# Token mixer of a Macaron block: its front in two strands, gate and convolutions as strands, PSUM banks from one pool, keys in quarters

## Chip, core and metric

The kernel runs on one core of a Trainium2 chip. The metric is the device time of one execution in microseconds (us). PE is the TensorE matmul engine (PEld its weight loads), DVE VectorE, ACT ScalarE, POOL GpSimd, SP the SyncE queue that issues most transfers. Each engine works through its own instructions in order; semaphores make it wait for the others.

## What is computed

A Macaron block on x of 16 x 256 tokens of 128 numbers: half a mixture-of-experts layer, a token mixer, half a mixture-of-experts layer, each on a layer norm and added to x. All in float32.

```python
x = x + 0.5 * ffn(layernorm(x))
x = x + attn(layernorm(x))
x = x + 0.5 * ffn(layernorm(x))
```

The mixer `attn`, cut to what matters (4 heads of 32, chunks of 32 tokens):

```python
q, k, v = (silu(causal_conv4(h @ W)) for W in (Wq, Wk, Wv))
beta = sigmoid(h @ Wb)
q, k = l2norm(q), l2norm(k)
attn = -(k * beta) @ k.T * strict_lower          # per chunk, 32 x 32
for i in range(1, 32):
    attn[i, :i] += attn[i, :] @ attn[:, :i]      # inverse of a triangular system
attn = attn + eye(32)
u, w = attn @ (v * beta), attn @ (k * beta)
for each chunk:                                  # scan over 8 chunks
    a_loc = q @ k.T * incl_lower
    u = u - w @ S
    delta = q @ S + a_loc @ u
    S = S + k.T @ u
ms = mix(conv3(v), conv15(v), conv31(v)) @ channel_mixer_w
features = concat(h, mean|ms|, mean|delta|, mean|v|)
wts = softmax(gelu(features @ W1 + b1) @ W2 + b2)
o = wts[0] * ms + wts[1] * delta + wts[2] * v
return rmsnorm(o) @ Wo
```

## The kernel before

The program has three stages. The first routes all tokens, scatters them by expert through DRAM and runs 2 x 8 expert passes (L456 to L533). The second is the token mixer (L670 to L1178). The third repeats the expert passes for the second half layer, whose routing has been done inside the mixer.

The mixer treats the tokens in four groups (g = 0 to 3) of 4 sequences x 256 tokens. For each group there are five Python generators, called strands:

- `front` (L724): adds the last expert output to x (load y from `back`, L731), layer norm, transposes into hT, projections pj for keys and queries (L719, four taps each, two halves), beta, the norms pn of k and q from squares sq. Then, in the same strand, the keys are spread by heads into `kh` by small copies on SP (L801, two halves of four copies), the products pa (L813) are masked into acomp and alc, acomp is transposed to sys, `inv` is set to the identity on POOL (L839) and the 32 x 32 systems are inverted on DVE, column after column (L846, L851, 31 steps of two instructions). Last, tcomp goes to the zero-padded tz on ACT (L872), and pw and pu (L881) give wT and uT.
- `values` (L890): projection of v, 16 copies that lay v out with lags in `vlag` (L909), transposition to vtok.
- `scan` (L918): 8 chunks, each pc, ui, pS, S, po, with DVE between the matmuls.
- `mixing` (L990): the lagged convolutions as 26 rounds of four 32-column matmuls (pms, L1010), channel mixing pk, then the gate: features, hidden layer ph, logits plg, softmax, the weighted sum o, norm, oT, output matmul pyo added to x.
- `routing` (L1168): routing of the group for the second expert stage, and 16 indirect stores by POOL (`dispatch`, L435).

What sets the order: a planner, `Weave.run` (L92), takes the steps of all strands, with an estimated length per step from `pe`, `dve`, `act` and `dma` (L62 to L75), and issues at each turn the step that could start first; the compiler's scheduler takes the resulting program as its order of preference. `("wait", key)` holds a strand until another has called `weave.mark(key)`; `("hold", "R")` takes the one bank R. In `front`, the wait for `("front", g - 1)` at L727 stands ahead of everything, and that mark is set at L888, after pw and pu of the group before. The products pa wait for the scan of the group before (L794).

[...]In the mixer F has two (front and values), V two (mixing), and C, O (scan outputs), S (scan state) and R (routing and logits) one each (L670). In SBUF, the ring f4 (two buffers, front) holds y, xn, sq, acomp, kb and vb, the ring b4 (three) the tiles of mixing; kq has two buffers, alc, sys, inv, wT, uT and ktok one.

Of the kernel before, what the change touches and what calls it, by code (L numbers as in the profile page):

```python
# [26 lines left out]
VPAD = 28  # L27
# [34 lines left out]
def pe(cols, *after):  # L62
    return PE, max(0.06, 0.0014 * cols), after


def dve(n, *after):
    return DVE, 0.15 + 0.00104 * n, after


def act(n, *after):  # L70
    return ACT, max(0.45, 0.12 + 0.00091 * n), after
# [6 lines left out]
class Weave:  # L78
# [4 lines left out]
    def __init__(self):  # L83
        self.done, self.held = {}, set()
# [4 lines left out]
    def let_go(self, key):  # L89
        self.held.discard(key)  # L90

    def run(self, strands):  # L92


        free, now = {}, [[s, next(s)] for s in strands]

        def start(step):
            if step[0] == "wait":
                return 0.0 if step[1] in self.done else None
            if step[0] == "hold":  # L100
                return 0.0 if step[1] not in self.held else None
            engine, _, after = step

            return max(
                [free.get(engine, 0.0)]
                + [t + (0.0 if e == engine else 0.2) for e, t in filter(None, after)]
            )

        while now:
            at, i = min((t, i) for i, (_, step) in enumerate(now) if (t := start(step)) is not None)  # L110
            strand, step = now[i]
            if step[0] == "wait":
                answer = self.done[step[1]]
            elif step[0] == "hold":
                self.held.add(step[1])
                answer = None
            else:
                engine, length, _ = step

                free[engine] = at + (0.1 if engine == SP else length)  # L120
# [8 lines left out]
def macaron_kernel(ctx: ExitStack, tc: tile.TileContext, x_in, consts, wts, w1b, wexp, out):  # L129
# [7 lines left out]
    banks = {}  # L137

    def psum_for(phase, **tags):
# [4 lines left out]
        for tag, n in tags.items():  # L144
            banks[tag] = (p, n)

    def bank(tag, name):
        p, n = banks[tag]
        return p.tile([P, 512], F32, tag=tag, bufs=n, name=name)

# [6 lines left out]
    psum_for("1", A=4, B=2, R=1)  # L157
# [23 lines left out]
    weave = Weave()  # L181
# [72 lines left out]
    def transposed(dst, src, tag, name, t=None, by_batch=False):  # L254


        for half in range(2):
            pt = bank(tag, f"pt_{name}_{half}")
            for q in range(4):
                t1 = yield pe(128, t)  # L260
# [7 lines left out]
            else:  # L268
                nc.scalar.copy(dst[:, half * 512 : (half + 1) * 512], pt)
        return t2  # L270

    def by_token(dst, mov, w32, p, at0, n, t=None):

        for b in range(4):
            t1 = yield pe(n / 4, t)
# [10 lines left out]
    class Routing:  # L286


        def __init__(self, layer, pool, bufs):
# [7 lines left out]
            self.last = None  # L297
# [5 lines left out]
        def route(self, g, tag, t=None):  # L303
# [10 lines left out]
            yield "hold", "R"  # L314
            pr = bank("R", f"pr_{nm}")
            t = yield from by_token(
                lgt.rearrange("p n r -> p (n r)"), lambda b: xnT[:, b, :],
                gate32.rearrange("p i e -> p (i e)"), pr, 0, L, t,
            )
            weave.let_go("R")  # L320
# [51 lines left out]
            yield "hold", "R"  # L372
            pp = bank("R", f"pp_{nm}")
# [46 lines left out]
            weave.let_go("R")  # L420

        def in_order(self, sent):

            sent = sent.ins if hasattr(sent, "ins") else sent
# [112 lines left out]
    for g in range(NG):  # L537
        weave.run([r1.route(g, "A")])
# [131 lines left out]
    psum_for("2", F=2, V=2, C=1, O=1, S=1, R=1)  # L670
# [7 lines left out]
    vlag = ap_.tile([P, 4, 4, VPAD + L], F32, name="vlag")  # L678
    nc.gpsimd.memset(vlag[:, :, :, : VPAD + 3], 0.0)
    kh = ap_.tile([P, H, 4 * P], F32, name="kh")  # L680
# [9 lines left out]
    def fring(name):  # L690
        return big("f4", name, 2)

    def bring(name):
        return big("b4", name, 3)
# [16 lines left out]

    def projection(g, w, half, t):

        pj = bank("F", f"pj{w}_{g}_{half}")
        hT = held[g]["hT"]
        for i in range(KQ):
            t1 = yield pe(512, t)
# [6 lines left out]
    def front(g):  # L724
# [4 lines left out]
        t = yield dma(3.0)  # L729
# [6 lines left out]
        t = yield from layernorm(xn, g, f"a{g}", t)  # L736
        hT = f["hT"] = hTs[g % 2]
        t = yield from transposed(hT[:, :, KQ - 1 :], xn, "F", f"a{g}", t, by_batch=True)
        weave.mark(("hT", g), t)

        kq = f["kq"] = ap_.tile([P, 2, NC * P], F32, tag="kq", bufs=2, name=f"kq_{g}")
        tk = {}
        for i in range(2):
            for half in range(2):
                pj, t1 = yield from projection(g, i, half, t)
                tk[i, half] = yield act(512, t1)
                nc.scalar.activation(
                    by_chunk(kq[:, i, half * 512 : (half + 1) * 512]), pj, AF.Silu
                )

        pb = bank("F", f"pb_{g}")
# [3 lines left out]
            wb32.rearrange("p i h -> p (i h)"), pb, 0, L, t,  # L755
        )
        beta = small("beta", [NC, H], f"beta_{g}", 1)
# [5 lines left out]
        pn = bank("F", f"pn_{g}")  # L763
        r32 = small("r32", [2, NC, 32], f"r32_{g}", 1)
        for i in range(2):
            sq = fring(f"sq{i}_{g}").rearrange("p (b l) -> p b l", b=4)
            t1 = yield act(1024, tk[i, 1])
            nc.scalar.activation(
                sq.rearrange("p b (n c) -> p b n c", c=CH), by_chunk(kq[:, i, :]), AF.Square
            )  # L770
            t1 = yield from by_token(
                r32[:, i].rearrange("p n r -> p (n r)"), lambda b: sq[:, b, :],
                blk32.rearrange("p i h -> p (i h)"), pn, i * L, L, t1,
            )
        r2 = small("r2", [2, NC, H], f"r2_{g}", 1)
# [15 lines left out]
        weave.mark(("bv", g), t2)  # L791


        yield "wait", ("scan", g - 1)  # L794
        acomp = fring(f"acomp_{g}")
        alc = f["alc"] = ap_.tile([P, NC, H, CH], F32, tag="alc", name=f"alc_{g}")
        for half in range(2):
            for h in range(H):
                rows = slice(h * DH, (h + 1) * DH)
                t1 = yield dma(2.5, tk[0, half])  # L800
                nc.sync.dma_start(  # L801
                    out=kh[rows, h, :], in_=kq[rows, 0, half * 512 : (half + 1) * 512]
                )
            for q in range(2):
                n0 = 4 * half + 2 * q
                pa = bank("F", f"pa_{g}_{n0}")
                for n in (n0, n0 + 1):
                    for h in range(H):
                        t2 = yield pe(64, t1)
                        c0 = ((n - n0) * H + h) * 2 * CH  # L810
                        for b in range(4):
                            at0 = (n % 4) * P + b * CH
                            nc.tensor.matmul(  # L813
                                pa[b * CH : (b + 1) * CH, c0 : c0 + 2 * CH],
                                lhsT=kh[:, h, at0 : at0 + CH],
                                rhs=kq[:, :, n * P + b * CH : n * P + (b + 1) * CH],
                                start=True, stop=True,
                            )
                pv = pa.rearrange("p (m i e) -> p m i e", i=2, e=CH)
                ta = yield dve(256, t2, tb)  # L820
                nc.vector.tensor_tensor(
                    m32(acomp)[:, n0 * H : (n0 + 2) * H, :], pv[:, :, 0, :],
                    nbk[:, n0 : n0 + 2, :].rearrange("p n h -> p (n h)").unsqueeze(2).to_broadcast(
                        [P, 2 * H, CH]
                    ),
                    ALU.mult,
                )
                yield dve(256)
                nc.vector.tensor_tensor(
                    alc[:, n0 : n0 + 2].rearrange("p n h c -> p (n h) c"), pv[:, :, 1, :],  # L830
                    incl32.unsqueeze(1).to_broadcast([P, 2 * H, CH]), ALU.mult,
                )

        sys_ = big("sys", f"sys_{g}").rearrange("p (e c) -> p e c", e=CH)
        yield dve(1024)
# [442 lines left out]
```

## Time and profile before

Three executions took 1179.99, 1186.2 and 1199.26 us; the median is 1186.2 us.

| | |
|---|---|
| profiled execution | 1185.7 us, its span 1183.7 us, mean TensorE clock 0.891 |
| busy over the span | PE 918.1 us (78%), DVE 494.8 (42%), ACT 353.8 (30%), POOL 296.3 (25%) |
| routing and expert stage 1 | 0 to 346 us |
| token mixer | 346 to 931 us: first group to 444, then some 133 us for each further one, last scan ends at 864 |
| expert stage 2 | 931 to 1184 us |
| costliest mixer groups | pms L1010 112.3 us, pj L719 94.9 us (PE), inverse L846 and L851 42.3 and 42.4 us (DVE) |

In windows of the trace, each row gives for a stretch the busy time of each engine with its instructions, the granted TensorE clock (1.00 is full speed) and the share of time in which the transfer engines were busy. The chain of waits follows the end of the program back from each instruction to what released it. "issue" is time in which an engine waited for nothing that the profile shows.

### The profile page before, as it was taken

The page shows a single profiled execution, that of the slowest core. Times are in us where ns is not written, and L with a number is a line of the kernel's source. Part 1 is how long each engine was busy: PE and PEld are TensorE (multiplying, and loading weights), DVE is VectorE, ACT ScalarE, POOL GpSimd, SP SyncE. Part 2 cuts the span into 40 slices and gives each one's busy share as a digit, 9 for nine tenths or more (in the row PEclk, how much of TensorE's full clock was granted, in tenths as well). Part 3 has the DMA queues.
Part 4 walks back from the last instruction along what each step waited for, and adds up shares of the span by engine and source line. Part 5 has one row for each costly group of instructions (what it writes and reads, how often), then busy time and mean ns, then how long its engine had stood idle before and what let it go on. Part 6 is the DMA issues. An engine that isn't in the chain of part 4 may idle for free.

```text
span 1183.7 us, 19481 instructions
## 1 busy us (share of the span) xinstructions
PE 918.1 (78%) x7721; PEld 613.5 (52%) x7721; DVE 494.8 (42%) x1346; ACT 353.8 (30%) x694; POOL 296.3 (25%) x312
## 2 busy tenths in 40 slices
PE   4348888999949858977597958977644699989992
PEld 2236666777733434443454435443432477767772
DVE  7422323443330563359325644359243133343332
ACT  6213212222214133622345223622232122222220
POOL 2623555333340000002300050002201433323331
PEclk9668999999988987989698978989675799999997
DMA  9451643533110301030103011030002233342314
GB/s 331 170 214 61 190 164 125 201 110 94 57 36 9 82 1 28 9 73 17 40 10 81 2 37 28 13 69 18 22 1 86 69 108 101 100 161 90 102 32 153
DMA packets 40491, 97.43 MB, mean 82 GB/s; under 512 B 8560, under 2 KB 17239, under 8 KB 40400
## 3 DMA queue, kind: packets, MB, share of 16 engines
q1 hardware_dynamic: 29888, 76.78, 21.1%
q0 software_dynamic: 9216, 16.87, 4.3%
q10 hardware_dynamic: 1296, 2.54, 0.6%
q8 instruction: 61, 1.00, 0.3%
q14 instruction: 30, 0.25, 0.1%
HBM read 47.65 MB, written 40.29 MB: 74 GB/s over the span
## 4 chain that ended last, share of the span: by engine, by line
PE 56%; DVE 20%; issue 12%; DMA 5%; ACT 2%; POOL 2%; another core or an unknown queue 1%; SPq 0%; POOLq 0%; DVEq 0%; ACTq 0%
PE pg L494 11%; PE py L511 11%; PE pu L499 11%; PE pj L719 8%; DVE inv L851 3%; DVE add L846 3%; PE pms L1010 3%; DMA y<-back 3%; PE ptx L483 1%; POOL disp L439 1%; ACT tz L872 1%; DVE ye L515 1%; PE pw L881 1%; PE pu L881 1%
## 5 line engine op out<-in xcount | busy, mean ns | idle before, releaser
L439 POOL DMA_INDIRECT disp<-row,send x128 | 128.4, 1003 | 474.5 <-DVE inv L851 337.6
L523 POOL DMA_INDIRECT back<-ye,xd x160 | 156.3, 977 | 312.6 <-DVE ye L515 259.6
L505 DVE TENSOR_TENSOR hT<-pu,sg 128x320 f32<-128x320 f32 x256 | 125.5, 491 | 181.5 <-PE pu L499 117.0
L494 PE MATMUL pg<-xdT,we 128*128 128x320 f32 x512 | 185.3, 444 | 1.2 <-issue 1.1
L499 PE MATMUL pu<-xdT,we 128*128 128x320 f32 x512 | 181.9, 437 | 4.3 <-issue 3.6
L504 ACT ACTIVATE sg<-pg 128x320 f32<-128x320 f32 x256 | 111.8, 437 | 197.8 <-PE pg L494 133.6
L511 PE MATMUL py<-we,hT 128*128 128x128 f32 x1280 | 151.1, 276 | 8.9 <-DVE hT L505 8.4
L511 PEld LDWEIGHTS py<-we,hT 128*128 128x128 f32 x1280 | 149.0, 192 | 16.0 <-DVE hT L505 9.9
L499 PEld LDWEIGHTS pu<-xdT,we 128*128 128x128 f32 x512 | 97.7, 192 | 48.0 <-issue 8.0
L494 PEld LDWEIGHTS pg<-xdT,we 128*128 128x128 f32 x512 | 95.8, 193 | 43.7 <-ACT xdT L486 5.2
L1010 PE MATMUL pms<-vlag,lagw 128*32 128x512 f32 x832 | 112.3, 594 | 3.8 <-DMA vlag<-vbl 3.2
L719 PE MATMUL pj<-hT,wc 128*128 128x512 f32 x192 | 94.9, 624 | 1.2 <-ACT hT L264 0.9
L486 ACT COPY xdT<-ptx 128x384 f32<-128x384 f32 x32 | 15.3, 480 | 185.7 <-PE ptx L483 164.1
L515 DVE TENSOR_TENSOR ye<-py,xd 128x384 f32<-128x384 f32 x64 | 31.4, 491 | 94.1 <-PE py L511 92.0
L483 PE MATMUL ptx<-cst,xd 128*128 128x128 f32 x160 | 31.2, 298 | 47.9 <-DMA xd<-disp 36.9
L1010 PEld LDWEIGHTS pms<-vlag,lagw 128*32 128x32 f32 x832 | 34.1, 109 | 59.8 <-issue 54.9
L945 DVE TENSOR_TENSOR ui<-pc,cst 128x512 f32<-128x512 f32 x32 | 22.1, 691 | 91.4 <-PE pc L930 50.6
L719 PEld LDWEIGHTS pj<-hT,wc 128*128 128x128 f32 x192 | 33.9, 194 | 36.3 <-issue 31.8
L483 PEld LDWEIGHTS ptx<-cst,xd 128*128 128x128 f32 x160 | 19.1, 149 | 55.7 <-DMA xd<-disp 19.2
L881 PE MATMUL pw<-tz,kb 128*32 128x128 f32 x256 | 14.4, 398 | 38.0 <-ACT tz L872 38.0
L846 DVE TENSOR_TENSOR add<-sys,inv 128x31 f32<-128x31 f32 (+15 forms) x124 | 42.3, 341 | 3.5
L851 DVE TENSOR_TENSOR inv<-inv,add 128x31 f32<-128x31 f32 (+15 forms) x124 | 42.4, 342 | 3.2
(211 smaller groups left out, 978.1 us busy)
## 6 DMA issues: line engine op xcount, KB each, us to landing
we<-in_wexp_dram SPq DMA_DIRECT2D x32, 768.0 KB
disp<-empty SPq DMA_DIRECT2D x4, 2620.0 KB
xd<-disp SPq DMA_DIRECT2D x32, 327.5 KB
back<-zero SPq DMA_DIRECT2D x4, 2048.0 KB
y<-back SPq DMA_DIRECT2D x16, 512.0 KB
back<-ye,xd POOLq DMA_INDIRECT x160
x<-in_x_dram SPq DMA_DIRECT2D x4, 512.0 KB
disp<-row,send POOLq DMA_INDIRECT x128
```

The source lines that it names most:

```text
L439: sent = nc.gpsimd.indirect_dma_start(out=self.slots[k][g * NC + n], out_offset=bass.IndirectOffsetOnAxis(ap=send[:, k, n : n + 1], axis=0 ...
L483: nc.tensor.transpose(pt[:, i * P : (i + 1) * P], xd[:, j, :D], ident)
L494: nc.tensor.matmul(pg[:, :w], lhsT=we[:, f * P : (f + 1) * P], rhs=xdT[:, s0 : s0 + w], start=True, stop=True,)
L499: nc.tensor.matmul(pu[:, :w], lhsT=we[:, FF + f * P : FF + (f + 1) * P], rhs=xdT[:, s0 : s0 + w], start=True, stop=True,)
L504: nc.scalar.activation(sg, pg[:, :w], AF.Silu)
L505: nc.vector.tensor_tensor(hT[:, f, s0 : s0 + w], pu[:, :w], sg, ALU.mult)
L511: nc.tensor.matmul(py[:, i * P : (i + 1) * P], lhsT=hT[:, f, j * P : (j + 1) * P], rhs=wo[:, f, :], start=(f == 0), stop=(f == 3),)
L523: sent = nc.gpsimd.indirect_dma_start(out=self.rows[k][e * JS + j], out_offset=bass.IndirectOffsetOnAxis(ap=xd[:, j, D : D + 1].bitcast(I3 ...
L719: nc.tensor.matmul(pj, lhsT=wc[:, w, i, :], rhs=hT[:, :, l0 : l0 + P], start=(i == 0), stop=(i == KQ - 1))
L846: nc.vector.tensor_tensor(add, sys_[:, j, k:].unsqueeze(2).to_broadcast([P, r, k]), iv[:, j, :k].unsqueeze(1).to_broadcast([P, r, k]), ALU ...
L851: nc.vector.tensor_tensor(iv[:, k:, :k], iv[:, k:, :k], add, ALU.add)
L1010: nc.tensor.matmul(pm_[i][32 * tile_ : 32 * tile_ + 32, :], lhsT=lagw[:, q, u, :], rhs=vlag[:, q, :, l0 : l0 + 128], start=first, stop=last,)
```

## The change

The mixer's strands are cut anew, now eight per group: `scan`, `systems` (keys by head, pa, inverse, pw and pu), `tokens` (ktok, kb, vb), `front` (up to the norms), `values`, `gate`, `routing`, `conv`. They are named in the order of their priority in the planner (0.1 us per place). The five banks of F, V and R become one pool G; each step that takes a bank names it with `take`, and `let_go` gives it back with the planned time. The planner's costs are other numbers. Keys are spread in quarters through two buffers. `inv` is filled by ACT. v is written with its zero padding into a persistent vbl and copied whole. k and the two alternating q share one tile, kqq. Rings: f4 3 (was 2), b4 2 (was 3), alc 2 (was 1), row 1 (was 2), part one half at a time. The gate's sum o is written into mtok. Routing in the first stage takes its bank from A.

```diff
 def pe(cols, *after):
-    return PE, max(0.06, 0.0014 * cols), after
+    return PE, 0.02 + 0.00168 * cols, after
+def pe4(cols, *after):
+    return PE, 0.06 + 0.0017 * cols, after
 def dve(n, *after):
-    return DVE, 0.15 + 0.00104 * n, after
+    return DVE, 0.155 + 0.00104 * n, after
 def act(n, *after):
-    return ACT, max(0.45, 0.12 + 0.00091 * n), after
+    return ACT, max(0.27, 0.13 + 0.0009 * n), after
...
-            at, i = min((t, i) for i, (_, step) in enumerate(now) if (t := start(step)) is not None)
+            ready = [(start(step), i) for i, (_, step, _) in enumerate(now)]
+            _, at, i = min((t + 0.1 * now[i][2], t, i) for t, i in ready if t is not None)
...
-                free[engine] = at + (0.1 if engine == SP else length)
+                free[engine] = at + (0.6 if engine == SP else length)
...
+    def take(tag, name):
+        t = yield "hold", tag
+        return bank(tag, name), t
...
-    psum_for("1", A=4, B=2, R=1)
+    psum_for("1", A=4, B=2)
...
-    psum_for("2", F=2, V=2, C=1, O=1, S=1, R=1)
+    psum_for("2", G=5, C=1, O=1, S=1)
...
-    vlag = ap_.tile([P, 4, 4, VPAD + L], F32, name="vlag")
+    vlag = ap_.tile([P, 4, 4 * (VPAD + L)], F32, name="vlag")
+    vbl = ap_.tile([P, 4, VPAD + L], F32, name="vbl")
...
-    kh = ap_.tile([P, H, 4 * P], F32, name="kh")
+    kh = ap_.tile([P, 2, H, 2 * P], F32, name="kh")
...
     def front(g):
         yield "wait", ("front", g - 1)
...
         t = yield from layernorm(xn, g, f"a{g}", t)
+        yield "wait", ("hidden", g - 2)
         hT = f["hT"] = hTs[g % 2]
...
+        tk = yield "wait", ("ktok", g - 1)
+        yield "wait", ("pa", g - 1)
+        yield "wait", ("scan", g - 2)
...
+        weave.mark(("front", g), t2)
+
+    def systems(g):
+        yield "wait", ("systems", g - 1)
+        tq = []
+        def spread(i):
             for h in range(H):
                 rows = slice(h * DH, (h + 1) * DH)
-                t1 = yield dma(2.5, tk[0, half])
+                t = yield dma(2.5, tk, tq[i - 2] if i > 1 else None)
                 nc.sync.dma_start(
-                    out=kh[rows, h, :], in_=kq[rows, 0, half * 512 : (half + 1) * 512]
+                    out=kh[rows, i % 2, h, :], in_=kT[rows, i * 256 : (i + 1) * 256]
                 )
+            return t
+        tk = yield "wait", ("k", g, 0)
+        there = [(yield from spread(0)), (yield from spread(1))]
+        tk = yield "wait", ("k", g, 1)
+        tb = yield "wait", ("front", g)
...
         inv = big("inv", f"inv_{g}")
-        nc.gpsimd.memset(inv, 0.0)
-        nc.gpsimd.memset(inv[:, 0 : CH * CH : CH + 1], 1.0)
+        yield act(1024)
+        nc.scalar.copy(inv, nought[:, 0:1].to_broadcast([P, CH * CH]))
+        t = yield act(32)
+        nc.scalar.copy(inv[:, 0 : CH * CH : CH + 1], nought[:, 1:2].to_broadcast([P, CH]))
...
-        weave.mark(("front", g), t2)
+        weave.mark(("systems", g), t3)
+
+    def tokens(g):
+        yield "wait", ("scan", g - 1)
+        t = yield "wait", ("k", g, 1)
+        ktok = f["ktok"] = big("ktok", f"ktok_{g}")
+        t1 = yield from transposed(ktok, kT.rearrange("p (n t) -> p n t", t=P), "G", f"k{g}", t)
+        weave.mark(("ktok", g), t1)
+        yield "wait", ("acomp", g)
+        for name, src, by, key in (("kb", "ktok", "nbk", "ktok"), ("vb", "vtok", "bv", "vtok")):
+            t1 = yield "wait", (key, g)
+            to = f[name] = fring(f"{name}_{g}")
+            t = yield dve(1024, t1)
+            nc.vector.tensor_tensor(m32(to), m32(f[src]), over(f[by]), ALU.mult)
+        weave.mark(("kb", g), t)
...
                 nc.sync.dma_start(
-                    out=vlag[32 * j : 32 * j + 32, q, :, VPAD + j :],
-                    in_=vbl[32 * q : 32 * q + 32, :, : L - j],
+                    out=vlag[32 * j : 32 * j + 32, q, j:],
+                    in_=vbl[32 * q : 32 * q + 32].rearrange("p b l -> p (b l)")[
+                        :, : 4 * (VPAD + L) - j
+                    ],
                 )
...
     def scan(g):
-        t = yield "wait", ("front", g)
-        yield "wait", ("gate", g - 1)
+        t = yield "wait", ("systems", g)
+        yield "wait", ("delta", g - 1)
...
-    def mixing(g):
+    def conv(g):
-        yield "wait", ("out", g - 1)
         t = yield "wait", ("vlag", g)
+        yield "wait", ("conv", g - 1)
...
+    def gate(g):
+        yield "wait", ("out", g - 1)
...
-    r2_ = Routing(2, rt, 2)
+    r2_ = Routing(2, rt, 1)
...
+    STRANDS = (scan, systems, tokens, front, values, gate, routing, conv)
...
-    weave.run([strand(g) for g in range(NG) for strand in (scan, front, values, mixing, routing)])
+    weave.run([(i, strand(g)) for g in range(NG) for i, strand in enumerate(STRANDS)])
```

## The prediction

> **What bounds the kernel now.** I read the page's 40 slices first, for stages, then the windows table, the chain of waits, and the timeline of one period. The expert layers fill 70 to 331 us and 931 to 1153 us. The change's new code runs between, in the token mixer (346 to 931 us). Earlier it only takes the routing bank from pool A. Columns below: stretch, length, busy us (instructions) of PE, PE weight load, DVE, ACT, POOL, then granted TensorE clock, DMA share, GB/s.
>
> ```profile
> 359.00:444.00 85.00, 67.77 (x712) 34.84 (x716) 36.09 (x86) 21.70 (x36) 1.10 (x2) 0.92 0.15 32
> 444.00:581.00 137.00, 109.02 (x1308) 59.01 (x1304) 66.87 (x188) 48.81 (x84) 17.73 (x18) 0.85 0.13 32
> 581.00:714.00 133.00, 105.45 (x1290) 57.23 (x1285) 67.06 (x188) 50.09 (x85) 17.73 (x18) 0.87 0.14 33
> 714.00:847.00 133.00, 105.29 (x1288) 57.09 (x1283) 67.07 (x188) 50.09 (x85) 16.61 (x16) 0.87 0.14 33
> 847.00:864.00 17.00, 12.23 (x405) 8.96 (x401) 8.98 (x13) 2.77 (x8) 0.00 (x0) 1.00 0.01 3
> 864.00:931.00 67.00, 24.63 (x157) 17.44 (x158) 22.70 (x70) 18.04 (x30) 14.55 (x15) 0.60 0.19 64
> ```
>
> A period of 133 us per group has 105 us of PE, 67 us of DVE and 50 us of ACT. No engine is full, so a chain sets the period. Inside one period:
>
> ```profile
> 627.00:632.00 5.00, 5.00 (x34) 1.96 (x32) 2.00 (x7) 4.89 (x7) 0.00 (x0) 1.00 0.00 0
> 637.00:642.00 5.00, 1.51 (x95) 1.18 (x83) 5.00 (x8) 2.65 (x4) 0.00 (x0) 1.00 0.94 191
> 642.00:647.00 5.00, 2.31 (x10) 2.10 (x11) 2.86 (x8) 1.16 (x3) 0.00 (x0) 0.52 0.85 179
> 692.00:697.00 5.00, 0.00 (x0) 0.00 (x0) 3.11 (x7) 1.60 (x3) 3.78 (x5) 0.64 0.17 54
> 702.00:707.00 5.00, 2.91 (x11) 0.58 (x8) 0.00 (x0) 0.00 (x0) 4.04 (x5) 0.50 0.16 54
> ```
>
> The chain of waits over that period names what passes (start, us, what):
>
> ```profile
> 662.84 1.89 DVE sys L836
> ...
> 693.41 1.92 DVE tcomp L854
> ...
> 697.94 1.94 PE pw L881 x32
> ```
>
> From the next stretch of the same view: load, normalize, transpose, project, strictly one after another.
>
> ```profile
> 714.13 3.55 DMA y<-back
> ...
> 719.53 1.55 DVE st_a L237 x8
> ...
> 729.81 2.84 PE pj L719 x6
> ```
>
> So the front of group g+1 starts when g's last inverse product is out (714.1). From there 15.7 us pass before a projection runs, under a scan that fills PE by half; then projections, scan and gate crowd PE (597 to 632 us, full); then the inverse holds DVE for some 30 us, and PE runs out of convolutions before it ends. That is the shape to break.
>
> **The Trainium skill.** "Perfetto Trace Analysis", Optimization Strategy, says kernels whose most contended engine changes over time may gain by interleaving those regimes: the case here (PE full at 627, DVE full at 637). Its Identifying the Most-Contended Engine warns that matmul busy share overstates nearness to the limit; here that share falls to nothing at 692, so the holes at least are real. "TensorE: Matmul & The Clock Gate", What's actually happening, has the clock halve after an idle window: the table agrees (1.00 in full windows, 0.50 to 0.64 at 692 to 707). "ScalarE: Activation LUTs", What ACT_TABLE_LOAD costs, gives 1283 ns plus a drain; the rows show 1283 ns, 36 times over the mixer, and no gap of a drain's size after (load at 733.62, Silu at 734.92).
>
> **The change part by part.**
>
> *Front split from systems.* front(g+1) now waits for keys of g used up (ktok, pa) and for scan(g-1), not for pw and pu of g. Its y load, layernorm and hT copies wait only for the front before and, for the ring of two hT, for the hidden layer of g-1. Nothing is removed: the same 24 projection matmuls (48 in the trace) and 62 DVE instructions of the inverse run per group. What can go is PE idle time. From hT(0) at 359 to the end of scan(3) at 864 PE is busy 400 of 505 us (sum of the first five rows, 399.8). Weighting each 5 us window's PE time by its clock gives 363 us at full clock, about 97 per inner group.
>
> Can the strands be late? A group's systems take, alone: first key quarters 4.5 us (four issues, 2.4 us, and landing), two more quarters behind them about 9, then from the first group's trace 403.6 (sys) to 441.0 (uT copied), 37 us: 51 us. A lone scan takes about 22 us (842 to 864), the gate to its sum 20 (865 to 885). These cycles, 51 and 42, are far under 97, so PE is next late, and I let it set the period.
>
> *Sum.* Wall = 363 / (share busy x clock). Now: 363/505 = 0.72 for the product. Full windows show 1.00 x 1.00; I take 0.93 x 0.96, since the strands still meet in-order queues: 407 us. *Scatters:* while POOL issues 16 indirect stores (1.28 us apart, 20.5 us), PE's pu matmuls crawl with "issue" ahead of them (566.9 to 575.3, again 699.6 to 708.2), about 8 us lost, three times. Nothing in the change thins them. With luck they fall under long convolutions (0), at worst all 24 us remain beside the 0.93; I add 10. So 417 against 505: 88 us less.
>
> *Tail.* 864 to 931 is gate(3), routing(3), 16 scatters, with nothing beside them: the same instructions, kept at 67 us. The start, 346 to 359, is also kept.
>
> *Keys in quarters.* 32 kh issues become 64, at 0.54 to 0.67 us of SP: +4.8 us of SP per group. Queued behind them on SP are y loads and 16 vlag copies (10.9 us per group); per period SP has some 21 of 100 us. The first two quarters start at k's two halves under the q projection; quarters 2 and 3 wait for pa(0), pa(1), then issue 2.4 plus landing: the vlag copy at 388.00 released PE 2.96 us later. Exposed at most 2 x 5 us on DVE's chain per group, 0 while PE has other work: 0 taken, 40 the bad end, and below nothing too: in the period shown the second half's keys were issued at 644.2, behind 16 vlag copies, so a gain of some 5 us per group stays possible.
>
> *vlag.* Still 16 copies, each one run of 4.5 KB per partition in place of four of 1 KB; no row shows it. The same 16 issues: 0, with -5 to +5 in all, as SP's issue time of 10.9 us sets it.
>
> *inv's fill from POOL to ACT.* 965+154 ns of POOL leave a queue where it stood behind scatters (572.8). On ACT 1.06 us (row osq, 1024 wide) plus 0.2, four times, 5 us in all; behind it are projection evictions, which PE awaits through a bank. ACT is at 51 of 105 us, so 0, at worst 5. Mixed strands will also switch ACT tables more: 36 loads now; 12 to 36 more cost ACT 15 to 46 us, hidden by the same slack, and partly the reason for 0.93.
>
> *Banks.* F, V, R (five) become one pool of five: same count, no instruction. A convolution half holds two and the logits one, leaving two for projections, as F had: 0, -5 to +10.
>
> *Rings.* f4 gets three buffers, b4 two, row one; o is written in place. kb and vb sit in two f4 buffers through the inverse, leaving one for y, xn and the squares in turn. Those are serial anyway: 0 to 15 us per period. One row buffer waits for the last scatters of g-1, a period earlier: 0; if routings come closer than 20.5 us, up to 20.
>
> *New costs and priorities* in the planner are no device work; they place instructions, at no cost of their own.
>
> **The rivals.** *Half an overlap.* The keys of g+1 wait for ktok(g), which waits for scan(g-1), and sq of q may wait for kb's buffer until pw is done. Then only load, layernorm and transposes hide: 15.7 us x 3 = 47, giving 1139. For it: single ktok, f4 of three. Against: the scan ends some 20 us into a 51 us chain. Chance 0.20, spread 1120 to 1180.
>
> *DVE's queue decides (slower).* Scan and inverse now share DVE for long. A ui or S at its head that awaits PE stops the group's 62 inverse instructions behind it, then tcomp, tz and pw. Now the waits for pc and pS average 1.4 us (71.6 us in 50, without the starts), longest 6.1. Sixteen per group at w lengthen the chain to 51 + 16w: under the present 133 up to w = 5.1, slower from there. At 6.1: 149 per period, 3 x 16 = +48, less some 12 that the first group still gains, 1222. Against: the mean is a quarter of this. Chance 0.06.
>
> *It does not do what it says:* dependencies keep the old order, 1186. PE's 80% speaks for little room; the empty windows against. Chance 0.04.
>
> **How the numbers follow.** The profiled execution was 1185.7 (span 1183.7 and 2.0 around it), the median 1186.2, so I subtract from the median: 1186 - 88 = 1098, chance 0.70. Its ends: 0.98 x 1.00 with no scatter loss, 370 us, gives 1051; 0.86 x 0.93 with 24 us, 478, gives 1159. Below 1062 PE would have to be full nearly throughout. 1062 to 1152 leaves out some 0.03 below, and the worst of the first case, a third of half an overlap, and the last two above: about 0.2. Two per cent (1162 and 1210) is what a measurement can tell here, as the three runs differ by 1.6%. Faster: 0.70 and three quarters of 0.20, 0.85; slower: most of 0.06, 0.05; same: 0.10.
>
> **What would show it.** A mixer of about 500 us from 346; PE at 9 tenths in most slices to scan(3), its clock at or near 1.00; projections of g+1 inside the inverse of g; y loads before pw; the tail still 67 us. The split is wrong if projections still begin after pu, or DVE waits for pc and pS rise past 3 us. The number is wrong if PE waits show ACT tables or "issue" in the new mixture.

## The result and the profile after

The changed kernel takes 1179.64 us in the median of 20 runs (1173.41 to 1185.67). The kernel before took 1189.28 us in 20 runs beside them. The ratio is 0.9923 [0.9901, 0.9944]: some 9 us less, where 88 were forecast. The profiled execution took 1176.96 us, its span 1175.2 us.

First the table by stretches of the trace after, cut at the ends of the four groups' systems (444, 535, 636, 764), the end of the last scan (811) and the last store (925). Columns as in the prediction.

```profile
357.00:444.00 87.00, 70.48 (x624) 32.92 (x617) 37.49 (x104) 32.40 (x54) 0.00 (x0) 0.86 0.17 42
444.00:535.00 91.00, 72.76 (x1133) 38.69 (x1131) 49.77 (x119) 26.43 (x50) 0.00 (x0) 0.89 0.16 38
535.00:636.00 101.00, 89.55 (x1229) 49.25 (x1229) 63.96 (x158) 43.45 (x77) 0.00 (x0) 0.97 0.15 35
636.00:764.00 128.00, 106.89 (x1282) 57.34 (x1281) 65.13 (x169) 45.82 (x77) 15.81 (x16) 0.91 0.13 32
764.00:811.00 47.00, 37.71 (x593) 24.45 (x592) 26.03 (x65) 18.63 (x32) 0.00 (x0) 0.82 0.01 2
811.00:925.00 114.00, 45.30 (x274) 26.43 (x269) 31.76 (x120) 25.41 (x46) 48.14 (x48) 0.66 0.17 57
```

The periods are 91, 101 and 128 us where they were some 133, and the last scan ends 54 us sooner (864.7 before, 811.0 after). So the groups do follow each other more closely. But the stretch behind the last scan, 67 us before, is now 114, and gives 46 us back. Its POOL column says why: 48 stores in it, where it had one group's 16. Before, the four bursts of stores began at 551.6, 684.4, 817.5 and 912.2; now at 688.1, 815.1, 853.6 and 904.7. PE has 45 us of work in the tail and not 25: the last convolution, which was done 49 us ahead of the end of the last scan, now ends 12 us behind it (823.1).

From the table of waits over the mixer (engine, line, releaser: us in total, times, longest):

```profile
DVE row L323 <- DMA disp<-row,send: 33.7, 2, 22.2
ACT part L1087 <- remote: 23.2, 2, 15.4
DVE acomp L860 <- remote: 21.8, 1, 21.8
```

The first is the copy of token numbers into the one row buffer: it waits until the stores of the group before have read that buffer, and everything behind it on DVE waits too. In the kernel before, with two row buffers, no such wait appears. The other two stand beside bursts of stores ("remote": the profile names no instruction that ended the wait). The kernel before has such waits of ACT beside its own bursts, 29.0 us in three (wT, L887). The 5 us windows of the first burst show what is behind the third:

```profile
685.00:690.00 5.00, 5.00 (x108) 2.49 (x110) 4.26 (x19) 2.11 (x3) 1.63 (x2) 1.00 0.20 53
...
700.00:705.00 5.00, 1.09 (x7) 0.63 (x7) 0.00 (x0) 0.00 (x0) 3.78 (x5) 0.72 0.16 54
705.00:710.00 5.00, 1.37 (x7) 0.49 (x7) 0.00 (x0) 0.00 (x0) 2.83 (x3) 0.50 0.16 54
```

PE gets through 7 matmuls in 5 us, with "issue" ahead of them, while DVE waits for these products, pa of group 3. Their last two sets of 64, with the projections between them, take 23 us here (689.5 to 712.5), and 4 us in the run without stores below (e2, 696.9 to 700.9). The stores end at 708.4, and from 711.0 PE runs at its old rate.

Three theories follow. **Starvation**: stores issued back to back by POOL slow PE and ACT. **Row**: the single row buffer holds DVE and ACT behind those stores. **Order**: gate and convolutions of early groups are planned too late, hold the one delta buffer, and let all routings pile up at the end.

### The profile page after: what moved, and what is told of

The parts are those of the page before. It is cut to its first block, busy times and chain, and to the rows that moved or that the text cites. A ratio compares the mean times of both kernels' runs of the same rounds, so it can differ in the third digit from the quotient of the medians.

```text
span 1175.2 us, 19559 instructions
## 1 busy us (share of the span) xinstructions
PE 912.7 (78%) x7721; PEld 608.6 (52%) x7721; DVE 499.5 (43%) x1346; ACT 356.5 (30%) x702; POOL 290.6 (25%) x307
## 3 DMA queue, kind: packets, MB, share of 16 engines
q1 hardware_dynamic: 25280, 77.83, 21.5%
## 5 line engine op out<-in xcount | busy, mean ns | idle before, releaser
L1078 PE MATMUL pms<-vlag,lagw 128*32 128x512 f32 x832 | 122.1, 607 | 19.2 <-DVE add L892 12.8
L740 PE MATMUL pj<-hT,wc 128*128 128x512 f32 x192 | 98.2, 640 | 0.3 <-issue 0.3
L851 PE MATMUL pa<-kqq,kh 128*32 128x64 f32 x1024 | 26.9, 237 | 20.8 <-issue 11.3
L273 PE MATMUL pt_r<-cst,row 128*128 128x128 f32 x64 | 18.3, 405 | 29.3 <-ACT row L261 15.1
```

Source lines behind the costliest of these rows:

```text
L740: nc.tensor.matmul(pj, lhsT=wc[:, w, i, :], rhs=hT[:, :, l0 : l0 + P], start=(i == 0), stop=(i == KQ - 1))
L1078: nc.tensor.matmul(pm_[i][32 * tile_ : 32 * tile_ + 32, :], lhsT=lagw[:, q, u, :], rhs=vl[:, q, :, l0 : l0 + 128], start=first, stop=last,)
```

## The experiments

The first twelve (e1 to e12) ran on two chips where the kernel before takes 1190.35 to 1191.09 us (beside the result it took 1189.28), "the first chips" below; the last six on two others, where it takes 1150.58 us (e13 to e15) and 1151.95 us (e16 to e18), "the faster chips". Ratios are to the kernel before, run beside each on the same chip; positions in a trace are compared from the first product pa of group 0 where two chips are involved.

**Stores left out.** Routing of groups 0 to 2 is worked out, but its stores are not made, in the changed kernel (e2) and in the kernel before (e3).

```diff
-        r2_.dispatch(g, 0)
-        r2_.dispatch(g, 1)
+        if g == NG - 1:
+            r2_.dispatch(g, 0)
+            r2_.dispatch(g, 1)
```

> The changed kernel without the indirect stores of routing for groups 0 to 2 of the mixer (the last group's 16 stay); the second expert stage then reads empty slots for those tokens, its instructions are the same. Scatter theory: the last pa group runs at once (the 21.8 us wait before acomp goes), PE's hole from 823 to 837 us closes, the row waits go too; 40 to 55 us less in all, about 1130. Row theory alone: 11 to 25 us less. Order theory alone (gate late because of its place in the order): 0 to 5 us less.

> The kernel before without the indirect stores of routing for groups 0 to 2 of the mixer. Scatter theory: the slow pu matmuls (three times about 8 us) run at full rate, so 20 to 26 us less than before, about 1165. If the stores only happen to lie beside a stall with another cause: 0 to 3 us less.

Measured: 1133.49 us, ratio 0.9545 [0.9502, 0.9587], and 1174.81 us, 0.99 [0.9837, 0.9963]. In the kernel before, the stores cost 12 to 16 us; in the changed one some 45 (0.9923 less 0.9545, of 1190). This takes away both a starving PE and a held row buffer, so it sizes the two together. The mixture and the tail of the changed kernel without stores:

```profile
363.00:799.00 436.00, 370.22 (x4856) 199.41 (x4856) 242.60 (x617) 167.36 (x289) 0.00 (x0) 0.91 0.13 32
799.00:882.00 83.00, 41.27 (x271) 24.63 (x269) 31.12 (x118) 25.38 (x45) 15.54 (x16) 0.71 0.15 53
```

The tail is 83 us and not 114. The mixture, from the first hT to the last scan, is 435 us and not 454.

**Row numbers on POOL, two row buffers.** e1 moves the copy alone to POOL; e5 takes two row buffers and, for the space, one alc buffer; e7 is the control for alc; e10 has all three.

```diff
-            nc.vector.tensor_copy(row[:, :, D].bitcast(I32), number[:, g, :])
+            nc.gpsimd.tensor_copy(row[:, :, D].bitcast(I32), number[:, g, :])
...
-    r2_ = Routing(2, rt, 1)
+    r2_ = Routing(2, rt, 2)
```

> The changed kernel with one instruction moved: the copy of the token numbers into the routing row (L323) is done by POOL instead of DVE, so that DVE no longer stands behind the stores of the group before. Row theory (the single row buffer stops DVE for 22.2 and 11.5 us): the waits of DVE for the disp landings vanish, the last gate's sum ends some 11 us earlier and the total falls by 10 to 14 us, to about 1167; the first wait brings nothing, as PE is held up beside it until 837 us. Scatter theory alone (PE is short of instructions while POOL stores): within 3 us of the changed kernel.

> Control: the changed kernel with alc in one buffer in place of two, as the next two need the space. All theories: 1176 to 1184 us, no difference from the changed kernel's 1180; anything above 1186 would be the price of that buffer and is to be taken off the next two.

> The changed kernel with two row buffers in place of one (alc one). Row theory: the waits of DVE's row copy for the scatters of the group before (33.7 us in two) are gone, the last gate runs 10 us sooner, 1166 to 1171. Scatter theory, and what the copy on POOL gave (2 us): the last group's bursts then only stand closer together, 1174 to 1181.

> The changed kernel with two row buffers (alc one), and the row numbers written by POOL, so that DVE waits for no store at all: the 22.1 us that DVE still waited with two buffers are gone. Row theory: another 8 to 15 us below the 1168 of two buffers alone, 1153 to 1160. Starvation theory: in that stretch (815 to 836) ACT and PE are starved too, and the last scans were done, so nothing more: 1164 to 1170.

Measured: e1 1177.81 us, 0.9878 [0.9823, 0.9933]; e7 1181.55 us, 0.9913 [0.9888, 0.9937], so alc costs nothing that shows; e5 1167.71 us, 0.9817 [0.9777, 0.9858]; e10 1162.8 us, 0.9771 [0.9732, 0.981]. Moving the copy alone gave 2 to 5 us, which is not clear of the noise, and a miss for the row theory as it stood: the layer norm on ACT writes the same buffer and came no sooner, 23.6 us behind the start of the burst (843.5) where it was 21.7 (836.8). With the buffer doubled 14 us came, and 19 with both, from the median of the control (11 and 17 by the ratios). With two buffers one wait was left, this time by the copy of group 3 for the stores of group 1:

```profile
DVE row L323 <- DMA disp<-row,send: 22.1, 1, 22.1
```

Taking this one away gave only some 5 us more, inside the intervals, because ACT was late in that stretch anyway (in e10 its two copies of convolution products still waited 18.2 us). The timeline of e1 shows it (start, length, engine, operation, idle before and releaser), with DVE held by nothing:

```profile
823.80 4.03 PE L1078 MATMUL pms<-vlag,lagw 128*32 128x512 f32 x28
832.19 0.59 ACT L1087 COPY part<-pms 128x512 f32<-128x512 f32 x1 [16.36 <-remote]
841.64 0.20 POOL L323 COPY row<-number 128x8 int32<-128x8 int32 x1 [1.47 <-DMA disp<-row,send]
842.83 0.58 ACT L1087 COPY part<-pms 128x512 f32<-128x512 f32 x1 [10.05 <-remote]
```

Both copies read products that were ready by 827.8, and the second runs 15 us later, 2.6 us after the burst's end at 840.2. The convolution itself is not slowed. In the changed kernel, too, the late copies and the held buffer end together, at 834.9 and 836.8, which fits that either alone, taken away, brought little there.

**Stores spaced out.** POOL does tiny fills between stores: twelve after each in the changed kernel (e8), six with two row buffers and the numbers on POOL (e9), six in the kernel before (e11).

```diff
                 self.in_order(sent)
+                if self.layer == 2 and g < NG - 1:
+                    for _ in range(6):
+                        self.in_order(nc.gpsimd.memset(self.idle, 0.0))
```

> The changed kernel with twelve tiny POOL fills after each of the 16 stores of groups 0 to 2, so that stores stand some 2.5 us apart in place of 1.28. If it is the density of the stores that starves PE: PE runs at nearly full rate beside them, and 20 to 40 us of the 46 that leaving them out gave come back: 1140 to 1160. If each store costs PE a fixed time wherever it stands: the same loss, longer drawn out, and the row buffer is held 20 us longer: 1178 to 1195.

> The same, with six tiny POOL fills after each store of groups 0 to 2, so that stores stand some 2.4 us apart. With twelve fills and one row buffer the products of group 3 ran at full rate beside the stores, and DVE then stood 112 us behind the row buffer. Starvation by back-to-back stores: with no row wait on DVE the products of group 3 are done some 14 us sooner than without fills, the last convolution is not held, 1140 to 1155. If the longer bursts give the loss back elsewhere (routings that queue up on POOL): 1165 to 1190.

> The kernel before, with six such fills after each store of groups 0 to 2. Starvation by back-to-back stores: pu of the next group runs at full rate beside them, and most of the 16 us that leaving the stores out gave come: 1174 to 1183. If each store costs PE the same wherever it stands: 1187 to 1195.

Measured: e11 1177.38 us, 0.9876 [0.9834, 0.9917]: spacing the stores gives the kernel before all that leaving them out gave. The same 32 products pu of group 1 can be read in three traces, first beside the stores of the kernel before:

```profile
566.85 1.77 PE L881 MATMUL pu<-tz,vb 128*32 128x128 f32 x17
568.98 0.65 PE L881 MATMUL pu<-tz,vb 128*32 128x128 f32 x3 [0.36 <-issue]
570.40 0.66 PE L881 MATMUL pu<-tz,vb 128*32 128x128 f32 x4 [0.78 <-issue]
572.54 1.09 PE L881 MATMUL pu<-tz,vb 128*32 128x128 f32 x4 [1.48 <-issue]
574.66 0.66 PE L881 MATMUL pu<-tz,vb 128*32 128x128 f32 x4 [1.03 <-issue]
```

Then without the stores (e3):

```profile
574.20 1.93 PE L881 MATMUL pu<-tz,vb 128*32 128x128 f32 x32
```

And beside stores 2.6 us apart (e11):

```profile
574.92 1.56 PE L885 MATMUL pu<-tz,vb 128*32 128x128 f32 x32
```

From the first to the last it is 8.5, 1.9 and 1.6 us. So it is density, not number.

e8 took 1238.57 us, 1.0402 [1.0367, 1.0437], far off its expectation of 1140 to 1195: PE was freed (pa of group 3 ended at 697.9 in place of 712.5), but bursts of 53 us held the single row buffer:

```profile
DVE row L324 <- DMA disp<-row,send: 112.2, 3, 54.8
ACT row L261 <- DMA disp<-row,send: 45.7, 1, 45.7
```

That is the row theory at its clearest: with longer bursts the wait grows to 112 us. e9 took 1160.1 us, 0.9732 [0.9685, 0.9779], only some 3 us under e10. The last scan came as early as without stores, but now POOL's own queue was the end: the last group's stores were ready at 863.2 and went out from 888.1, since some 40 us each for groups 1 and 2 stood ahead. Meanwhile almost nothing else ran:

```profile
860.00:880.00 20.00, 1.33 (x6) 1.23 (x6) 1.83 (x14) 0.00 (x0) 12.74 (x56) 0.50 0.09 27
880.00:900.00 20.00, 0.00 (x0) 0.00 (x0) 0.00 (x0) 0.00 (x0) 13.94 (x31) 0.50 0.12 37
```

**Other orders of the strands.** e4 names gate and routing behind tokens, then conv, and front and values last; e12, on top of e10, moves gate and routing ahead of front and values; its edit:

```diff
-    STRANDS = (scan, systems, tokens, front, values, gate, routing, conv)
+    STRANDS = (scan, systems, tokens, gate, routing, front, values, conv)
```

> The changed kernel with the strands in another order of priority: scan, systems, tokens, gate, routing, conv, front, values. Order theory (gate and conv too late, so delta is held, scans 2 and 3 stretch to 45 us, and the routings bunch at the end): first routing's stores before 620 us in place of 688, last scan under 30 us from uT, end of mixer 20 to 60 us earlier, 1120 to 1160. Against it: front comes later, the systems' periods grow past 120 us and the total is at or above the changed kernel's 1180.

> The changed kernel with two row buffers and the row numbers on POOL, and gate and routing named ahead of front and values (conv stays last). Order theory: routing of group 0 comes before the systems of group 3, the last three bursts stand less close, 8 to 15 us below the same without it. Against: gate waits for the convolutions, which stay last, and the tie breaks move little: within 5 us of it.

Measured: e4 1191.04 us, 0.9994 [0.9972, 1.0016]; e12 1200.49 us, 1.0094 [1.006, 1.0128], 38 us above e10. Routing of group 0 did come sooner in e12 (stores from 593 in place of 690), but its systems ended at 449, 556, 680 and 824: periods of 107, 124 and 144 us. In these two orders the theory that earlier gates would pay falls: what they gain in the tail the fronts lose.

**Two delta buffers.** e6 has two, the planner's wait unchanged; e14 also lets the scan start behind the gate of two groups before; e15 is e14 without the stores of the routing of groups 0 to 2.

```diff
-        yield "wait", ("delta", g - 1)
-        delta = f["delta"] = big("delta", f"delta_{g}").rearrange("p (n t) -> p n t", t=P)
+        yield "wait", ("delta", g - 2)
+        delta = f["delta"] = big("delta", f"delta_{g}", 2).rearrange("p (n t) -> p n t", t=P)
```

> The changed kernel with two delta buffers in place of one (alc one). If the delta held for the late gate is what keeps the last scans long: scan(3) takes 25 to 35 us in place of 52, ends some 15 to 20 us sooner, 1160 to 1168. If the stores beside PE and the late convolutions decide the end: the scan ends sooner, the tail behind it grows by as much, 1175 to 1183.

> The changed kernel with two delta buffers (alc one), and the planner's wait of the scan moved to the gate of two groups before; with two buffers but the old wait nothing moved (scan(3) 757.4 to 807.7). If that wait keeps the scans long: scan(3) takes 25 to 35 us in place of 52, and the last convolution takes the room; with the stores as they are 1165 to 1175. If not: 1176 to 1184.

> The same, without the stores of the routing for groups 0 to 2, to be read beside the 1133 of the changed kernel without those stores. If the scan's wait for the gate is what remains of the missing gain there: the last scan ends 15 to 20 us sooner, 1113 to 1123. If the last convolution sets the end whatever the scan does: 1127 to 1136.

Measured: e6 1180.19 us, 0.9918 [0.9882, 0.9953], against 1181.55 of the control: nothing. e14 1155.49 us, 1.0035 [1.0016, 1.0054], on a faster chip; on the other the changed kernel itself has 1.0018 (e16, below): nothing. e15 1111.9 us, 0.9666 [0.9639, 0.9693]. The scan of group 3 did shorten, from 55 to 33 us from its first product pc to its last delta, and in e15 it ended 20 us sooner than in e2 (389 and 409 us behind the first pa). But the second half of mtok of group 3 came 425 and 426 us behind it, and the last store 491 and 492. The held delta is not the cause. Beside e14, e15 sizes the stores on that chip: 43.6 us, as much as on the first chips, although e14 has no "remote" wait for a product or a copy. It has these:

```profile
DVE row L323 <- DMA disp<-row,send: 46.0, 3, 19.8
ACT row L261 <- DMA disp<-row,send: 12.2, 1, 12.2
```

So a loss of that size does not need starvation.

**The changed kernel on a faster chip, and the parts together.** e16 is the changed kernel itself. e13 and e18 are one kernel: two row buffers, numbers on POOL, and fills of six and four for groups 0 and 1 only, so that POOL is free for the last stores. e17 adds the last group's convolution named ahead of everything.

```diff
-                if self.layer == 2 and g < NG - 1:
-                    for _ in range(6):
+                if self.layer == 2:
+                    for _ in range((6, 4, 0, 0)[g]):
```

> As with six fills, two row buffers and the row numbers on POOL, but six fills after each store of group 0, four for group 1, none for groups 2 and 3. With six everywhere the stores of group 3 were ready at 863 us and went out at 888, since POOL was still busy with the longer bursts of groups 1 and 2. If POOL's queue is now the end: some 20 to 25 us less, 1136 to 1144. If the close burst of group 2 starves the last gate again: 1148 to 1162.

> The changed kernel itself once more, as the last three runs were on a chip where the kernel before takes 1150 us and not 1190, and where 286 and not 64 to 88 matmuls ran beside the first burst. If chips differ in how much back-to-back stores starve PE: where before takes 1190, ratio 0.99 and some 80 matmuls per burst; where before takes 1150, 200 and more beside the first burst, and a ratio of 0.98 to 1.00 all the same, since before gains too.

> Two row buffers, row numbers on POOL, stores spaced by six and four fills for groups 0 and 1, again, to stand beside the changed kernel on one chip. Starvation and row theory: where before takes 1190, 40 to 48 us below the changed kernel (as without the stores); where before takes 1150, 25 to 40.

> The same, with the convolutions of the last group named 3 us ahead of everything in the planner, and no longer last. If the last convolution sets the end (it ends after the last scan, mtok(3) some 17 us behind the scan's last output): 8 to 16 us below the same without it. If the scan then ends later by as much: within 5 us of it.

Measured: e13 1112.29 us, 0.9676 [0.964, 0.9713]; e16 1153.68 us, 1.0018 [1.0006, 1.003]; e18 1111.61 us, 0.965 [0.9631, 0.9669]; e17 1127.13 us, 0.9789 [0.9766, 0.9812]. So e18 beats both kernels, by 42 us the changed one and by 40 the one before, on that chip. On its chip the first burst of e16 did not starve PE:

```profile
674.40:694.60 20.20, 20.16 (x256) 9.97 (x258) 8.40 (x29) 2.76 (x5) 15.63 (x16) 1.00 0.19 58
```

PE is full, with 256 matmuls; the trace of the result has 89 in the same stretch. Beside the second burst (from 792.8) ACT copies the convolution products as they come, at 799.1 and 800.8, but its layer norm and DVE's copy then wait for the row buffer until 814.3, 21.5 us behind the burst's start and no sooner than in the trace of the result (21.7). The row waits of e16 in all; in e18 neither engine has one left:

```profile
DVE row L323 <- DMA disp<-row,send: 44.2, 3, 22.1
ACT row L261 <- DMA disp<-row,send: 13.0, 1, 13.0
```

44 us of DVE went, and 42 us of time. How much the fills add there wasn't run apart; nor was e18 run where stores starve PE. e17 missed: mtok of group 3 was ready 14 us sooner (775.9 and 790.4), but the last scan ended 13 us later (786.2 and 773.4), and the last store 12 us later. No single strand is late at the end of the mixture; they share what is there.

## Why the prediction was wrong

**Overlap: right in the size of the periods, wrong in its path.** y of the next group loads 73 to 89 us ahead of the last uT of the group before. But only the load and the layer norm are early. For group 2 the normalized xn comes at 475.8, ahead of the inverse of group 1 (from 482.3); its transposes come at 540.0 and its projections at 542.9, behind the last uT of group 1 and right behind the hidden layer ph of group 0:

```profile
534.11 0.60 ACT L925 COPY uT<-pu 128x512 f32<-128x512 f32 x1
...
537.80 1.02 PE L1145 MATMUL ph<-hT,aw 128*128 128x512 f32 x2
...
540.00 0.77 PE L273 MATMUL pt_a<-cst,xn 128*128 128x128 f32 x5
...
542.85 1.55 PE L740 MATMUL pj<-hT,wc 128*128 128x512 f32 x3
```

Group 3 does the same (uT to 636.2, ph of group 1 from 645.1, projections from 652.0), and without stores it is no different (e2: uT to 540.3 and 643.5, projections from 548.5 and 659.3). That is the sign the prediction had named for a wrong split, projections behind pu. The step that failed, as far as these positions show, is the wait for the ring of two hT: the prediction names it and gives it no price, and the hidden layer that frees the buffer belongs to a gate that comes late. Only group 1, which waits for no hidden layer, is early: its values are projected inside the inverse of group 0 (from 400.8), its keys from 432.7 (uT to 443.9).

The periods of 91 and 101 us are nevertheless under the some 107 that the forecast share gives (95 us of PE at full clock, cut from last uT to last uT, over 0.93 x 0.96), because they shrank elsewhere. From the last uT to the next group's first projection of keys it was 17, 14 and 14 us; now group 1 starts 11 us early, and groups 2 and 3 wait 8 and 16. From there to sys it was 67, 66 and 66 us, and is 50, 42 and 61 (42 in e2). From sys to the last uT it stayed at 51 to 53. The second period thus gains 24 us ahead of sys, of which 10 lie between the first acomp and sys (20.6 us before, 10.1 after): keys in halves had the third acomp 18 us behind the second (661.4 and 643.1). No run tried these parts apart.

Of the rivals, DVE's queue fell: its waits for pc and pS, without the starts, are 17.8 us in 20 and 12.6 us in 16, under 1 us each and not the 5.1 from which a slower kernel was to follow. Half an overlap came nearer to what groups 2 and 3 show, though by another wait, and they hide still less than it allows. That 1179.64 us lies at the edge of its spread is luck, as the tail put it there.

**The tail, "kept at 67 us": this step failed, and is the largest.** It measured 114. I had taken gate, routing and stores of groups 0 to 2 as done by then, as before. With conv last and everything pulled together, routing of group 0 stores at 688 (552 before), and groups 1 and 2 store at 815 and 854, behind the last scan. Without stores the tail is 83 us; the 16 left over go with the convolution that moved behind the scan (16.27 us of PE in its first 17). So 54 us were won ahead of it, and 46 lost in it.

**Rings: the row buffer was priced at 0, "if routings come closer than 20.5 us, up to 20".** The condition came true, and nothing had been set aside for it. The stores of group 1 were ready at 814.5 and the layer norm of group 2 at 814.4: DVE's copy waited 22.2 us, and the layer norm ran no sooner (836.8). Without stores (e2) those two routings are ready 20 us apart (802.1 and 822.3). The other 11.5 us are of a kind that the prediction lacked: the number copy of group 3 depends on nothing but the buffer and stands on DVE 14 us ahead of its own layer norm (876.7 and 890.9), so the gate behind it waits too. In all the single buffer costs 14 us (buffer) to 19 (copy too) on the first chips; on the faster ones DVE stood 44 us and the parts together gave 42.

**Scatters, 10 us more over the mixture:** mis-sized too, but less than it seemed. Of the 45 us that leaving out the stores gives, 14 to 19 is the row buffer. The mixture goes from 454 to 435 without them, 19 where I had 10; the rest falls in the tail. "With luck they fall under long convolutions (0)" was wrong, though the convolution of group 3 ran at its rate beside the stores (88 matmuls in 10.5 us): ACT's copies behind it waited 23.2 us.

**Sum: 0.93 x 0.96 was too high.** Weighting 5 us windows as there, PE's share times clock is 0.77 after, and 0.80 even without stores, against 0.72 before and 0.89 forecast: 435 us for 407, so 28 us of the miss are neither stores nor rows. Delta isn't the cause (e15), and two other orders and an earlier last convolution didn't help (e4, e12, e17). The share laid on each stretch of the kernel before shows where they lie. Without stores (e2) the first group takes 87 us, as before, and not 74: no group stands ahead of it to overlap with. The three periods take 91, 103 and 108, together 18 under their 107 each. The last scan, from its last uT, takes 47 (16 before) and not 13, with gates and the last convolution beside it; in e15 it took 23, but the work behind it grew by as much. So the share was wrong at the two ends. What would shorten the last one stays open; no run took the wait for hT away, by a third buffer or otherwise.

**The small terms cost nothing that shows.** Key quarters: PE waited 9.3 us in 5 for kh, no more, and the gain named as possible, some 5 us per group, looks like 10. ACT tables: 37 loads in place of 36, where I had feared 12 to 36 more. For vlag PE waited once, 6.3 us (3.2 before). ACT waits 15.6 us for the constants of inv, but ahead of its first work in the mixer (348.7). For banks no wait of size appears. None of these was tried apart.

**The number.** Of the 88 us, the tail takes 46 and the slower mixture 37 (454 for 417). That leaves 5; with a mixer that began 2 us sooner (344.4 and 346.7) and a second stage 1 us shorter it is 8, and the profiled executions differ by 8.7.

## What to carry to other kernels

When strands are overlapped more tightly, price the end anew: what was done early under the old order may now queue behind the last long strand, and the tail isn't "the same instructions". A wait that the split leaves in place, such as that for one of two hT buffers, must be priced by when the strand that ends it is planned. A ring cut to one buffer must be priced by who stands behind the instruction that waits for it on its engine, and not only by how often two users meet; a small copy that depends on nothing but the buffer can reach the head of the queue early and block there. Spread bursts of indirect stores, but only as far as POOL's queue has room before the last of them.

## What the runs showed of the hardware

Beside indirect stores 1.28 us apart, PE and ACT fell behind on the first chips with their inputs ready: 32 products pu took 8.5 us, where they took 1.9 without the stores and 1.6 beside stores 2.6 us apart, and ACT ran two copies 10 us apart. It doesn't hit all work: 88 matmuls of the last convolution took 10.5 us beside the second burst in the traces of the result and of e16, and 10.5 without stores (e2). That it is the supply of instructions that is slowed is argued from "issue" ahead of matmuls, not shown: the blocks of instructions in the trace of the result beside the first burst arrived in 0.5 to 1.6 us each, and without stores (e2) in 0.3 to 1.6.

It differs by chip. Where the kernel before takes 1151 to 1152 us, the first burst let 256 (e16) and 287 (e14) matmuls through in 20 us. In the expert stage of the changed kernel, a pass beside eleven stores in a row takes 16.9 us in the trace of the result and 14.2 in e16's (from its first store to that of the next pass), a pass beside five 14.2 in both. Four such passes make up some 10 of the 15.6 us by which the first products pa came sooner (366.7 and 382.3). That the change gives 0.9923 on the first chips and 1.0018 on a faster one fits this, as the kernel before then has its own 12 to 16 us back; it wasn't tried apart.
